# Gated cross-attention with a routed feed-forward: keys loaded in shuffled runs of 128 bytes and turned in 32x32 blocks on VectorE

## The chip, the cores and the metric

The kernel runs on one core of one Trainium2 chip. The time is the device time of one execution in microseconds (us). A profile of one execution stands beside it; times in it are counted from its first instruction. The engines are called as the profile calls them: PE (TensorE, matrix products; PEld is its loading of weights), DVE (VectorE), ACT (ScalarE), POOL (GpSimd), SP (the queue that issues most DMAs). SBUF is the on-chip memory, PSUM the accumulators that PE writes.

## What is computed

All data are float32. There are 32 batches of 128 tokens with 128 features.

```
q    = layernorm(x)                      # x: (32, 128, 128)
k, v = split(ctx, 2)                     # ctx: (32, 128, 256)
w    = softmax(q_h k_h / sqrt(8) + b + mask(seq_len))     # 16 heads of 8
x    = x + tanh(g_xattn) * (w v_h)
y    = layernorm(x)
x    = x + tanh(g_ffn) * sum over the 2 chosen of 8 experts of
       gate * (relu(y wi + bi + (y A_e) B_e) wo + bo)     # hidden 512, rank 16
```

`b` is one number per key, and the mask adds -1e12 to keys at or behind the batch's length.

## The kernel before, in words

**Tiles and groups.** A tile has 128 partitions. Batches come in groups of four: `load(g)` (L191) brings x, the keys and the values of a group (`xg`, `kg`, `vg`, 256 KB each) with one DMA each; group 0 comes in two parts, first batch 0 (`True`), then the other three (`False`, whose keys are issued from ACT, L202). x and keys arrive with tokens on partitions. `load(1)` and `load(2)` are issued ahead of the first steps, `load(3)` inside them, and one more at each group from the fifth on.

**Attention of one batch n**, by the names of the steps:

- `moments0` (L336, DVE) and `query_scale` (L326 to L331, POOL) make the layernorm's factors; `normalise` (L419, ACT) writes the scaled query into `qpad`, where every head has 16 columns: 8 features, and extra ones that carry the key's bias and, later, the row's maximum.
- `key_features` (L381) and `key_bias` (L389) write keys and bias into `kpad` in the same form. In the loop both are part of `group_keys` on POOL.
- `turn` (L444, PE) makes four 128x128 transposes by products with the identity: two of the keys, two of the queries. `turned` (L450, ACT) copies all four from PSUM into `kq`; `keys` (L430, POOL) multiplies the keys' half by a mask into `ks`, so that one strip of 32 rows holds two heads.
- `logits` (L469, PE) makes query times key for one half of the heads in strips of 32 rows, into the one PSUM tile `lg`; `max` (L479, DVE) takes each row's maximum from it. `again` (L488, PE) turns the maxima, `queries` (L495, DVE) adds them to the queries, and a second set of products (L508, PE), with keys on the rows, goes into the one PSUM tile `lt`. `exp` (L537, ACT) reads that, `attend` (L549, PE) multiplies by the values, `attended` (L557, ACT) copies, `result` (L564, PE) turns, `residual` (DVE) divides by the sum and adds x.
- `products` (L469 and L508) interleaves the logits of a batch with the second products of one two batches earlier.

The feed-forward of four batches (steps from `tokens` to `result_out`) runs in the same loop, one group behind. Its products are L620, L635, L726, L737 and L789.

**The order** is written out by hand, and each engine executes its instructions in that order. `START` (L38) lists all until batch 4, `PLAN` (L71) the eight half-ticks that repeat for every four batches, `END` (L117) the rest. Steps of `START` carry their own numbers; the number after a loop step's name is the half, the piece or the group offset. `idle` (L230) are products of zeros that keep PE busy while it would wait; `blank_keys`, `blank_queries` and `blank_values` (L267 to L282) are memsets of the padded tiles, of which there are two each; called in `START`, `blank_values` 0 and all others but `blank_values` 1 run on DVE. The second number of `key_features` and `key_bias` in `START` names the engine: 0 DVE, 1 ACT, 2 POOL.

## Time and profile before

| | before |
|---|---|
| time, median of 3 | 298.6 us (298.49 to 299.34) |
| span of the profiled execution | 296.7 us |
| what the median has beyond that span | 1.9 us |
| PE busy | 286.7 us (97%), 3476 instructions |
| DVE busy | 211.6 us (71%), 592 instructions |
| ACT busy | 162.8 us (55%), 287 instructions |
| POOL busy | 128.1 us (43%), 264 instructions |
| DMA | 9.86 MB in 19109 packets |

Only the span of the profiled execution is recorded, not a total time of its own; the median lies 1.9 us above it, and that is taken as what lies around it. The page of the profile gives busy times and counts of each engine, the span in 40 slices, the DMA queues, the chain of work that ended last with the share of each engine and line, and the costliest groups of instructions. The trace answers further: a timeline of an engine, who waited for whom, and the busy time of each engine in chosen stretches. A matmul's shown duration includes its way through the array, so two neighbours overlap; what one costs PE is the distance between two starts.

### The profile page before, as it was taken

What the parts mean: (1) busy time and instruction counts of PE and PEld (TensorE: products, weight loads), DVE (VectorE), ACT (ScalarE), POOL (GpSimd) and SP (SyncE); (2) the same over time, 40 slices, a digit from 0 to 9 for tenths busy, and PEclk for the clock granted to TensorE, in tenths of its full rate; (3) what the DMA queues carried; (4) which work ended last, traced back from release to release, by engine and by line L of the source; (5) the groups of instructions that cost most, each with busy time, mean ns of one, the idle gap of its engine ahead of it and who ended that gap; (6) DMA issues with size and microseconds to landing.
All of it is one profiled execution on the core that took longest, in us unless ns stands there. A gap on an engine that the chain in (4) does not pass through costs nothing.

```text
span 296.7 us, 8420 instructions
## 1 busy us (share of the span) xinstructions
PE 286.7 (97%) x3476; PEld 209.5 (71%) x3476; DVE 211.6 (71%) x592; ACT 162.8 (55%) x287; POOL 128.1 (43%) x264
## 2 busy tenths in 40 slices
PE   8698999999999999999999999999999999999996
PEld 8477876787666865688567865688666865686475
DVE  7986789788767886777766886777756785348524
ACT  2537675675656654674655644674655643653340
POOL 4792374263624436353634436343633035304620
PEclk9999999999999999999999999999999999999999
DMA  5990003000400000050001000010001000011001
GB/s 138 271 244 12 2 3 106 2 4 0 127 2 0 2 2 2 0 144 4 2 0 38 3 2 0 2 39 2 0 2 38 2 0 3 1 38 35 2 0 53
DMA packets 19109, 9.86 MB, mean 33 GB/s; under 512 B 1664, under 2 KB 18816, under 8 KB 19072
## 3 DMA queue, kind: packets, MB, share of 16 engines
q1 hardware_dynamic: 18384, 9.12, 11.1%
q8 instruction: 27, 0.44, 0.6%
q10 hardware_dynamic: 688, 0.21, 0.3%
q14 instruction: 10, 0.08, 0.1%
HBM read 7.24 MB, written 2.10 MB: 31 GB/s over the span
## 4 chain that ended last, share of the span: by engine, by line
PE 88%; DVE 5%; DMA 2%; ACT 1%; POOL 1%; issue 1%; SPq 0%; ACTq 0%
PE ph L737 26%; PE lg L469 13%; PE lt L508 11%; PE shared L549 10%; PE po L789 10%; PE pt L444 4%; PE pzt L726 3%; PE pz L635 2%; PE avt L564 2%; PE shared L488 2%; DMA len_i<-in_seq_len_dram 1%; DVE highest L479 1%; DMA xg<-in_x_dram 1%; PE px L620 1%; PE busy L230 1%
## 5 line engine op out<-in xcount | busy, mean ns | idle before, releaser
L479 DVE TENSOR_REDUCE highest<-lg 128x8 f32<-128x1024 f32 x64 | 77.8, 1218 | 20.0 <-PE lt L508 13.9
L537 ACT ACTIVATE e<-lt 128x1024 f32<-128x1024 f32 x64 | 65.6, 1025 | 35.1 <-PE lt L508 34.6
L508 PE MATMUL lt<-qm,ks 32*128 32x128 f32 x1024 | 74.2, 283 | 0.2 <-ACT e L537 0.2
L469 PE MATMUL lg<-ks,kq 32*128 32x256 f32 x512 | 71.0, 400 | 0.2
L508 PEld LDWEIGHTS lt<-qm,ks 32*128 32x128 f32 x1024 | 62.0, 186 | 2.2 <-issue 1.4
L430 POOL TENSOR_TENSOR ks<-kq,head_mask 128x512 f32<-128x512 f32 x32 | 33.3, 1042 | 64.1 <-ACT kq L450 64.0
L737 PE MATMUL ph<-zt,bt_sb 128*128 128x512 f32 (+1 forms) x128 | 58.3, 568 | 0.0
L469 PEld LDWEIGHTS lg<-ks,kq 32*128 32x128 f32 x512 | 42.9, 184 | 19.5 <-issue 11.5
L781 DVE SCALAR_TENSOR_TENSOR h<-ph,nbi,r 128x512 f32<-128x512 f32 (+1 forms) x32 | 22.7, 708 | 21.2 <-PE ph L737 20.8
L789 PE MATMUL po<-wo_sb,h 128*128 128x128 f32 x256 | 35.0, 283 | 0.0
L549 PE MATMUL shared<-e,values 128*32 128x128 f32 x1024 | 34.6, 276 | 0.2 <-ACT e L537 0.2
L789 PEld LDWEIGHTS po<-wo_sb,h 128*128 128x128 f32 x256 | 30.9, 191 | 2.3
L737 PE MATMUL ph<-xt,wi_sb 128*128 128x512 f32 (+1 forms) x64 | 32.3, 589 | 0.0
L767 ACT ACTIVATE r<-ph,bi_sb 128x512 f32<-128x512 f32 (+1 forms) x32 | 21.2, 663 | 19.6 <-PE ph L737 19.6
L737 PEld LDWEIGHTS ph<-zt,bt_sb 128*128 128x128 f32 x128 | 21.8, 190 | 14.1 <-issue 11.2
L549 PEld LDWEIGHTS shared<-e,values 128*32 128x32 f32 x1024 | 26.0, 109 | 6.0 <-issue 3.2
L714 POOL TENSOR_TENSOR zm<-z,hot 128x512 f32<-128x512 f32 (+1 forms) x18 | 17.4, 966 | 26.4 <-DVE hot L686 17.6
L450 ACT COPY kq<-pt 128x512 f32<-128x512 f32 x32 | 18.7, 586 | 10.1 <-PE pt L444 9.9
L557 ACT COPY avs<-shared 128x256 f32<-128x256 f32 x32 | 11.9, 371 | 17.4 <-PE shared L549 16.8
L495 DVE TENSOR_TENSOR qm<-kq,shared 128x256 f32<-128x256 f32 x32 | 13.2, 413 | 11.2 <-ACT avs L557 10.4
L419 ACT ACTIVATE qpad<-xg,sh_q,rs_q 128x128 f32<-128x128 f32 x32 | 14.9, 493 | 7.7 <-POOL sh_q L331 7.1
L733 ACT COPY zt<-pzt 128x512 f32<-128x512 f32 (+1 forms) x18 | 9.7, 537 | 15.0 <-PE pzt L726 15.0
(121 smaller groups left out, 386.6 us busy)
## 6 DMA issues: line engine op xcount, KB each, us to landing
vg<-in_ctx_dram SPq DMA_DIRECT2D x8, 256.0 KB, 4.7
xg<-in_x_dram SPq DMA_DIRECT2D x7, 256.0 KB, 4.0
kg<-in_ctx_dram SPq DMA_DIRECT2D x7, 256.0 KB, 4.4
out_dram<-y SPq DMA_DIRECT2D x7, 256.0 KB, 2.3
wi_sb<-in_wi_t_dram SPq DMA_DIRECT2D x1, 256.0 KB, 4.9
wo_sb<-in_wo_t_dram SPq DMA_DIRECT2D x1, 256.0 KB, 5.2
bt_sb<-in_b_t_dram SPq DMA_DIRECT2D x1, 256.0 KB, 4.6
xg<-in_x_dram SPq DMA_DIRECT2D x1, 192.0 KB, 4.3
```

The lines of the kernel that those rows point to most:

```text
L430: engine.tensor_tensor(dst, src.unsqueeze(2).to_broadcast([P, 2, HB, P]), head_mask.unsqueeze(1).unsqueeze(3).to_broadcast([P, 2, HB, P]), ...
L450: nc.scalar.copy(kq, T.pop("pt"))
L469: lambda r=slice(32 * s, 32 * s + 32), d=lg[:, s % 2, c], c=c: nc.tensor.matmul(d, lhsT=T["kq"][r, 2 + c, :], rhs=T["ks"][r, c], start=Tru ...
L479: nc.vector.tensor_reduce(highest[n % 2][:, :, DH : DH + 2].rearrange("p (s j) c -> p s c j", s=NS)[:, 2 * half : 2 * half + 2], lg, AX.X, ...
L508: lambda r=slice(32 * s, 32 * s + 32), d=lt[:, s % 2, c, j], c=c, j=j: nc.tensor.matmul(d, lhsT=T["ks"][r, c, j, :], rhs=T["qm"][r, c, :], ...
L537: nc.scalar.activation(e, lt.rearrange("p s c j q -> p (s c j) q"), AF.Exp)
L549: nc.tensor.matmul(shared[32 * j : 32 * j + 32, 0, half, :], lhsT=group[g]["v"][:, i, HH * c + HB * s + odd, :], rhs=e[:, 2 * j + odd, :], ...
L714: nc.gpsimd.tensor_tensor(zm.rearrange("p b (e r) -> p (b e) r", r=R), G["z"][:, :nb].rearrange("p b (e r) -> p (b e) r", r=R), G[f"hot{k} ...
L737: nc.tensor.matmul(G["ph", c], lhsT=weights[:, c * P : (c + 1) * P], rhs=rows[:, : G["nb"]].rearrange("p b t -> p (b t)"), **flags)
L767: nc.scalar.activation(r, G["ph", c], AF.Relu, bias=bi_sb[:, c : c + 1])
L781: nc.vector.scalar_tensor_tensor(G["h"][:, c, : G["nb"] * P], G.pop(("ph", c)), nbi[:, c : c + 1], G.pop(("r", c)), ALU.max, ALU.add)
L789: nc.tensor.matmul(po, lhsT=G["h"][:, c, i * P : (i + 1) * P], rhs=wo_sb[:, c, :], start=(c == 0), stop=(c == NFC - 1),)
```

## The change

Keys are no longer turned by PE. Their DMA is split into four, one for each strip of 32 partitions. Within strip s, partition 32s+c receives for every batch the four runs of 32 consecutive features number s (128 bytes) of the keys c, 32+c, 64+c and 96+c. So each 32x32 block of the padded keys needs only to be turned in place, which the new step `turn_keys` does with one VectorE transpose of 128x256 elements a batch into `kt`. `turn` keeps the two transposes of the queries, `turned` copies half as much into `qt`, and `keys` on POOL reads `kt`. The bias of the keys follows the new layout: it is loaded by four DMAs and computed for four blocks. The queries' heads are laid out in the order of the strips, so `attend` and `result` address them differently, with the same number of instructions. All three lists of steps are ordered anew.

```diff
START = [
-    ("blank_queries", 1), ("blank_keys", 1), ("moments0", 0), ("lengths",), ("biases",),
-    ("key_features", 0, 0, 1, 4), ("query_scale", 0, 0, 1), ("key_features", 0, 1, 0, 1),
-    ("moments0", 1), ("query_scale", 0, 1, 2), ("key_bias", 0, 1, 0, 1), ("normalise", 0),
-    ("turn", 0), ("key_bias", 0, 0, 1, 4), ("moments0", 2), ("turned", 0),
-    ("normalise", 1), ("moments0", 3), ("keys", 0), ("turn", 1), ("blank_values", 0), ("idle", 1),
-    ("products", (0, 0, False), (0, 1, False)), ("query_scale", 0, 2, 4), ("turned", 1),
-    ("moments0", 6), ("moments0", 4), ("keys", 1), ("moments0", 5), ("max", 0, 0), ("normalise", 2),
-    ("turn", 2), ("normalise", 3), ("max", 0, 1), ("turned", 2), ("turn", 3),
-    ("products", (1, 0, False)), ("keys", 2), ("tanh",), ("moments0", 7), ("turned", 3),
-    ("max", 1, 0), ("group_keys", 1), ("normalise", 5), ("products", (1, 1, False)), ("max", 1, 1),
-    ("again", 0), ("normalise", 4), ("idle", 2), ("products", (2, 0, False)), ("queries", 0),
-    ("idle", 1), ("products", (0, 1, True)), ("again", 1), ("max", 2, 0), ("exp", 0, 1),
-    ("turn", 4), ("queries", 1), ("products", (2, 1, False), (0, 0, True)), ("exp", 0, 0),
...
+    ("moments0", 0), ("lengths",), ("biases",), ("key_bias", 0, 1, 0, 1), ("moments0", 1),
+    ("moments0", 3), ("query_scale", 0, 0, 1), ("key_bias", 0, 0, 1, 4),
+    ("key_features", 0, 1, 0, 1), ("key_features", 0, 0, 1, 4), ("turn_keys", 0), ("turn_keys", 1),
+    ("normalise", 0), ("query_scale", 0, 1, 2), ("keys", 0), ("turn", 0), ("turned", 0),
+    ("normalise", 1), ("idle", 1), ("products", (0, 0, False), (0, 1, False)), ("moments0", 2),
+    ("blank_keys", 1), ("query_scale", 0, 2, 4), ("normalise", 3), ("moments0", 6), ("turn", 1),
+    ("keys", 1), ("normalise", 2), ("moments0", 5), ("load", 3), ("idle", 4), ("turn", 2),
+    ("turn_keys", 2), ("max", 0, 1), ("idle", 1), ("max", 0, 0), ("turned", 1), ("moments0", 7),
+    ("blank_values", 0), ("again", 0), ("products", (1, 0, False)), ("max", 1, 0), ("tanh",),
+    ("keys", 2), ("queries", 0), ("turned", 2), ("products", (1, 1, False)), ("max", 1, 1),
+    ("turn", 3), ("blank_values", 1), ("moments0", 4), ("products", (2, 0, False)), ("max", 2, 0),
+    ("products", (0, 1, True)), ("turned", 3), ("group_keys", 1), ("exp", 0, 1), ("turn_keys", 3),
+    ("group_values", 0), ("blank_queries", 1), ("again", 1), ("normalise", 5),
+    ("products", (2, 1, False), (0, 0, True)), ("normalise", 4), ("queries", 1), ("turn", 5),
+    ("max", 2, 1), ("turn_keys", 4), ("idle", 2), ("exp", 0, 0), ("moments0", 10), ("keys", 3),
+    ("turn", 4), ("products", (3, 0, False), (1, 1, True)), ("again", 2), ("exp", 1, 1),
+    ("attend", 0), ("normalise", 6), ("moments0", 11), ("keys", 4), ("attended", 0), ("max", 3, 0),
+    ("moments0", 8), ("queries", 2), ("turn_keys", 5), ("products", (3, 1, False), (1, 0, True)),
+    ("turned", 4), ("keys", 5), ("max", 3, 1), ("turn_keys", 6), ("result", 0), ("exp", 1, 0),
+    ("products", (4, 0, False), (2, 1, True)), ("residual", 0), ("again", 3), ("attend", 1),
+    ("max", 4, 0), ("queries", 3), ("turned", 5), ("exp", 2, 1), ("keys", 6), ("attended", 1),
+    ("moments0", 9), ("products", (4, 1, False), (2, 0, True)), ("moments1", 0), ("normalise", 7),
+    ("result", 1), ("max", 4, 1), ("residual", 1), ("turn", 6), ("output_bias",), ("exp", 2, 0),
+    ("moments1", 1), ("products", (5, 0, False), (3, 1, True)), ("again", 4), ("exp", 3, 1),
+    ("group_values", 1), ("scale", 0), ("max", 5, 0), ("turned", 6), ("attend", 2),
+    ("products", (5, 1, False), (3, 0, True)), ("attended", 2), ("token", 0, 1), ("queries", 4),
+    ("token", 0, 0), ("exp", 3, 0), ("result", 2), ("tokens", 0), ("idle", 1), ("max", 5, 1),
+    ("group_keys", 2), ("residual", 2), ("idle", 1), ("moments1", 2),
 ]
...
 PLAN = [
     [
...
+        ("again",), ("logits", 0), ("tokens_sb", 1), ("moments0",),
     ],
     [
...
+        ("turn_keys",), ("attend",), ("project", 1, 0), ("max", 0), ("gates", 1, 0), ("exp", 1),
+        ("attended",), ("project", 1, 1), ("queries",), ("project_sb", 1, 0), ("gates", 1, 1),
+        ("out", 2, 2), ("result",), ("keys",), ("logits", 1), ("scores", 1), ("result_out", 2, 2),
+        ("exps", 1), ("residual",), ("project_sb", 1, 1), ("turn",), ("normalise",),
+        ("softmax", 1), ("turned",), ("exp", 0), ("out", 2, 1), ("max", 1), ("choice", 1, 0),
+        ("result_out", 2, 1), ("moments1",),
     ],
     [
...
+        ("common", 1, 1), ("turn",), ("turned",), ("masked", 1, 0), ("normalise",), ("logits", 0),
+        ("exp", 1), ("max", 0), ("attend",), ("choice", 1, 1), ("features", 1, 0), ("attended",),
+        ("common", 1, 0), ("again",), ("features_sb", 1, 0), ("masked", 1, 1), ("result",),
+        ("residual",), ("turn_keys",), ("keys",),
     ],
     [
...
+        ("logits", 1), ("features", 1, 1), ("own", 1, 1), ("moments0",), ("max", 1), ("own", 1, 0),
+        ("features_sb", 1, 1), ("relu", 1, 1), ("common", 1, 3), ("queries",), ("exp", 0),
+        ("relu", 1, 0), ("own", 1, 3), ("moments1",),
     ],
     [
...
+        ("second", 1, 1), ("logits", 0), ("relu", 1, 3), ("weight", 1), ("sum", 1, 1),
+        ("bias", 1, 1), ("again",), ("moments0",), ("bias", 1, 2), ("normalise",), ("turn",),
+        ("exp", 1), ("second", 1, 0), ("attend",), ("max", 0), ("logits", 1), ("turned",),
+        ("turn_keys",),
     ],
     [
...
+        ("sum", 1, 0), ("attended",), ("bias", 1, 0), ("exp", 0), ("queries",), ("result",),
+        ("max", 1), ("common", 1, 2), ("own", 1, 2), ("residual",), ("keys",), ("moments1",),
     ],
     [
...
+        ("normalise",), ("second", 1, 3), ("group_values", -1), ("again",), ("relu", 1, 2),
+        ("bias", 2, 3),
     ],
     [
...
+        ("out", 2, 3), ("result_out", 2, 3), ("scale", 0), ("logits", 0), ("turn_keys",),
+        ("max", 0), ("attend",), ("exp", 1), ("sum", 1, 3), ("keys",), ("turn",), ("second", 1, 2),
+        ("attended",), ("token", 0, 0), ("token", 0, 1), ("logits", 1), ("moments0",), ("turned",),
+        ("sum", 1, 2), ("queries",), ("max", 1), ("result",), ("token", 0, 2), ("group_keys", -2),
+        ("residual",), ("token", 0, 3), ("out", 1, 0), ("result_out", 1, 0), ("exp", 0),
+        ("tokens", 0), ("moments1",),
     ],
 ]
...
         bs = slice(g * GB + part.start, g * GB + part.stop)
         nc.sync.dma_start(out=xg[:, part, :], in_=x[bs].rearrange("b s d -> s b d"))
         keys = nc.scalar if first is False else nc.sync
-        keys.dma_start(out=kg[:, part, :], in_=ctx_kv[bs, :, 0:D].rearrange("b s d -> s b d"))
+        for s in range(NS):
+            keys.dma_start(
+                out=kg[32 * s : 32 * s + 32, part, :].rearrange("c n (b r) -> c n b r", r=32),
+                in_=ctx_kv[bs, :, 32 * s : 32 * s + 32].rearrange("n (b c) r -> c n b r", c=32),
+            )
         if first is not True:
             bs = slice(g * GB, (g + 1) * GB)
...
 
     len_i = const.tile([P, B], I32, name="len_i")
     nc.scalar.dma_start(out=len_i, in_=seq_len.to_broadcast([P, B]))
-    b_key = const.tile([P, 1], FP, name="b_key")
-    nc.scalar.dma_start(out=b_key, in_=b_col)
+    b_key = const.tile([P, NS], FP, name="b_key")
+    for s in range(NS):
+        nc.scalar.dma_start(
+            out=b_key[32 * s : 32 * s + 32, :], in_=b_row.rearrange("o (b c) -> c (o b)", c=32)
+        )
     load(0, True)
...
     nc.vector.tensor_copy(row, row_i)
-    pidx = const.tile([P, 1], FP, name="pidx")
-    nc.vector.tensor_copy(pidx, pidx_i)
+    pidx = const.tile([P, NS], FP, name="pidx")
+    nc.gpsimd.iota(pidx, [[32, NS]], base=0, channel_multiplier=0, allow_small_or_imprecise_dtypes=True)
+    nc.vector.tensor_scalar(pidx, pidx, row, None, ALU.add)
 
     head_mask = const.tile([P, HB], FP, name="head_mask")
...
-        kpads.append(const.tile([P, GB, H, HS], FP, name=f"kpad{i}"))
-        qpads.append(const.tile([P, GB, H, HS], FP, name=f"qpad{i}"))
+        kpads.append(const.tile([P, GB, NS, NS, HS], FP, name=f"kpad{i}"))
+        qpads.append(const.tile([P, GB, 2, NS, HB, HS], FP, name=f"qpad{i}"))
         values.append(const.tile([P, GB, H, 32], FP, name=f"values{i}"))
 
...
         for c in range(2):
-            engine.memset(kpads[i][:, :, c * HH : (c + 1) * HH, DH + c], 1.0)
+            engine.memset(kpads[i][:, :, :, HB * c : HB * c + HB, DH + c], 1.0)
 
     def blank_queries(engine, i):
         engine.memset(qpads[i], 0.0)
-        engine.memset(qpads[i].rearrange("p b h c -> p (b h) c")[:, :, DH + 2], 1.0)
+        engine.memset(qpads[i].rearrange("p b c s j e -> p (b c s j) e")[:, :, DH + 2], 1.0)
 
...
-        nc.vector.tensor_scalar(bias_key, len_f, pidx, MASK_VALUE, ALU.is_le, ALU.mult)
-        nc.vector.tensor_scalar(bias_key, bias_key, b_key, None, ALU.add)
-        nc.vector.tensor_tensor(bias_key, bias_key, some, ALU.mult)
+        def wide(t, axis):
+            return t.unsqueeze(axis).to_broadcast([P, B, NS])
+
+        nc.vector.tensor_tensor(bias_key, wide(len_f, 2), wide(pidx, 1), ALU.is_le)
+        nc.vector.scalar_tensor_tensor(
+            bias_key, bias_key, MASK_VALUE, wide(b_key, 1), ALU.mult, ALU.add
+        )
+        nc.vector.tensor_tensor(bias_key, bias_key, wide(some, 2), ALU.mult)
 
...
         G = record(g)
         copy = (nc.vector.tensor_copy, nc.scalar.copy, nc.gpsimd.tensor_copy)[engine]
         copy(
-            G["k"][:, lo:hi].rearrange("p b h c -> p (b h) c")[:, :, 0:DH],
+            G["k"][:, lo:hi].rearrange("p n b h c -> p (n b h) c")[:, :, 0:DH],
             G["kg"][:, lo:hi].rearrange("p b (h e) -> p (b h) e", e=DH),
         )
...
         copy(
-            record(g)["k"][:, lo:hi, :, DH + 2],
-            bias_key[:, n].unsqueeze(2).to_broadcast([P, hi - lo, H]),
+            record(g)["k"][:, lo:hi, :, :, DH + 2].rearrange("p n b h -> p (n b) h"),
+            bias_key[:, n].rearrange("p n b -> p (n b)").unsqueeze(2).to_broadcast(
+                [P, (hi - lo) * NS, NS]
+            ),
         )
 
     def query_scale(g, lo=0, hi=GB):
...
         G = group[g]
         nc.scalar.activation(
-            G["q"][:, i, :, 0:DH], G["xg"][:, i, :].rearrange("p (h e) -> p h e", e=DH),
+            G["q"][:, i, :, :, :, 0:DH],
+            G["xg"][:, i, :].rearrange("p (s c j e) -> p c s j e", c=2, j=HB, e=DH),
             AF.Identity, scale=G["rs"][:, i : i + 1], bias=G["sh"][:, i : i + 1],
         )
...
         g, i = divmod(n, GB)
         G = group[g]
-        pt = small([P, 4, P], f"pt{n}")
-        for s, t in enumerate((G["k"], G["q"])):
-            for c in range(2):
-                nc.tensor.transpose(pt[:, 2 * s + c, :], half_of(t, i, c), ident)
-        batch[n] = dict(pt=pt)
+        pt = small([P, 2, P], f"pt{n}")
+        for c in range(2):
+            heads = G["q"][:, i, c].rearrange("p s j e -> p (s j e)")
+            nc.tensor.transpose(pt[:, c, :], heads, ident)
+        batch.setdefault(n, {})["pt"] = pt
 
     def turned(n):
         T = batch[n]
-        kq = bat.tile([P, 4, P], FP, tag="kq", name=f"kq{n}", bufs=5)
-        nc.scalar.copy(kq, T.pop("pt"))
-        T["kq"] = kq
+        qt = bat.tile([P, 2, P], FP, tag="qt", name=f"qt{n}", bufs=5)
+        nc.scalar.copy(qt, T.pop("pt"))
+        T["qt"] = qt
+
+    def turn_keys(n):
+
+        g, i = divmod(n, GB)
+        kt = bat.tile([P, 2, P], FP, tag="kt", name=f"kt{n}", bufs=3)
+        nc.vector.transpose(
+            kt.rearrange("p c (b t) -> p b c t", t=32),
+            group[g]["k"][:, i].rearrange("p b (c j) e -> p b c (j e)", j=HB),
+        )
+        batch.setdefault(n, {})["kt"] = kt
 
     def keys_by_head(n):
         ks = bat.tile([P, 2, HB, P], FP, tag="ks", name=f"ks{n}", bufs=5)
-        spread(nc.gpsimd, ks, batch[n]["kq"][:, 0:2, :])
+        spread(nc.gpsimd, ks, batch[n].pop("kt"))
         batch[n]["ks"] = ks
 
 
...
-                    d, lhsT=T["kq"][r, 2 + c, :], rhs=T["ks"][r, c], start=True, stop=True
+                    d, lhsT=T["qt"][r, c, :], rhs=T["ks"][r, c], start=True, stop=True
                 )
                 for c in range(2)
...
-                    s, c = 2 * half + j // 2, j % 2
                     nc.tensor.matmul(
                         shared[32 * j : 32 * j + 32, 0, half, :],
-                        lhsT=group[g]["v"][:, i, HH * c + HB * s + odd, :], rhs=e[:, 2 * j + odd, :],
+                        lhsT=group[g]["v"][:, i, HH * half + HB * j + odd, :], rhs=e[:, 2 * j + odd, :],
                         start=(odd == 0), stop=(odd == 1),
                     )
...
         avt = small([P, 4, P], f"avt{n}")
         for half in range(2):
-            nc.tensor.transpose(
-                avt[:, 0:2, 64 * half : 64 * half + 64].rearrange("p c (s e) -> p s c e", e=32),
-                batch[n]["avs"][:, half, :], ident,
-            )
+            nc.tensor.transpose(avt[:, half, :], batch[n]["avs"][:, half, :], ident)
         batch[n]["avt"] = avt
 
```

Where the diff shows "...", lines are left out: the rest of the old `START`, the old `PLAN`, both `END`s, and changes of shape that only follow the new layout.

## The prediction

> **What bounds the kernel now.** I read the page first, then the busy time by stage, then PE's timeline, then who waits on SP's queue. The page and the stages:
>
> ```profile
> span 296.7 us, 8420 instructions
> PE 88%; DVE 5%; DMA 2%; ACT 1%; POOL 1%; issue 1%; SPq 0%; ACTq 0%
> ```
> ```profile
> core 0: us, PE busy (x) PEld busy (x) DVE busy (x) ACT busy (x) POOL busy (x), PEclk, DMA share, GB/s
> 0.00:11.04 11.04, 8.08 (x43) 7.30 (x43) 8.43 (x31) 3.72 (x8) 6.05 (x24) 1.00 0.74 192
> 11.04:39.16 28.12, 25.52 (x381) 20.36 (x380) 22.02 (x49) 16.68 (x29) 16.46 (x32) 1.00 0.37 101
> 39.16:250.72 211.56, 211.13 (x2716) 151.46 (x2715) 158.35 (x438) 125.20 (x217) 92.94 (x178) 1.00 0.07 19
> 250.72:296.70 45.98, 42.00 (x341) 30.41 (x340) 22.78 (x77) 17.21 (x34) 12.68 (x30) 1.00 0.07 21
> ```
>
> The stages are: until the first logits, the rest of `START`, the loop, `END`. In the loop PE is busy 211.13 of 211.56 us: there PE's own work sets the pace, and DVE has 25% to spare. Before 39.16 it is otherwise; PE waits there although `idle` products fill part of the gaps.
>
> PE's timeline at one `turn` among other full-size products:
>
> ```profile
> 134.24 1.05 PE L789 MATMUL po<-wo_sb,h 128*128 128x128 f32 x8
> 135.13 0.38 PE L444 MATMUL pt<-ident,kpad 128*128 128x128 f32 x2
> 135.34 0.38 PE L444 MATMUL pt<-ident,qpad 128*128 128x128 f32 x2
> 135.56 0.38 PE L564 MATMUL avt<-ident,avs 128*128 128x128 f32 x2
> ```
>
> Starts are what counts: the keys' pair costs 135.34 - 135.13 = 0.21 us, the queries' 0.22, so one transpose 0.11.
>
> SP's waits:
>
> ```profile
> SPq L217 <- DMA len_i<-in_seq_len_dram: 1.5, 1, 1.5
> SPq L314 <- DMA vg<-in_ctx_dram: 0.6, 1, 0.6
> SPq L201 <- DMA wi_sb<-in_wi_t_dram: 0.5, 1, 0.5
> SPq L203 <- DMA wo_sb<-in_wo_t_dram: 0.5, 1, 0.5
> ```
>
> Number the DMAs in program order: 1 `len_i`, 2 `b_key`, 3 and 4 x and keys of batch 0, 5 to 7 the rest of group 0, 8 and 9 the gates (L216, L217), and so on. L217 (9) waits for `len_i` (1), L314 (20) for the values of group 1 (12), x of group 2 (21) for `wi_sb` (13), its keys (22) for `wo_sb` (14). Each DMA that waits, waits for the eighth before it. I read eight slots in turn out of that: more DMAs at the start mean later DMAs.
>
> **The loop: what PE saves.** `turn` loses two transposes a batch, 0.218 us. The loop turns batches 7 to 31, 25 of them: 25 x 0.218 = **5.45 us**. The number of PE blocks is the same in both `PLAN`s (I count 8 of `products`, 4 of `attend` and 8 of full-size work between them), so no switch is gained or lost; I take nothing for it. A period of four batches (112.31 to 145.91 in the chain, 33.60 us) should become 33.60 - 0.87 = 32.73.
>
> **The loop: what must fit beside it.**
>
> - The DVE transpose is in no row. The nearest are the copy of 128x384 (353 ns), `qm` of 128x256 (413 ns) and the memset of 1024 elements (912 ns, so 0.23 us for 256). I take 0.35, nearest in shape; the lower end is 0.23, the upper 1.2, what the slowest step of a batch, L479 with 1218 ns, takes. DVE has 24.9 us in a period; with four transposes 26.3 of 32.73, at the upper end 29.7. It is in DVE's queue ahead of `max` twice, once of those in time that DVE waits for the product anyhow. By PE's order the second logits of the first half-ticks come 4.5 us into the period, and that `max` would be done at 3.1: 1.4 us of room, which even 1.2 us leaves.
> - ACT's `turned` falls from 586 to about 371 ns (the row of the 128x256 `avs`); POOL's `ks` stays at 1042. Both are cover, and gain nothing.
> - Tight places: `choice` ends on DVE at about 8.6 us of the period, POOL's `masked` (1.06) at 9.8, and `features` is due on PE at 10.1; the next pair is as close (12.8 and 13.1). `max` before the third `products` ends at 7.4, due at 8.0. They fit by 0.3 to 0.6 us, so I take no stall; if all three miss by 0.3 us, 7 periods lose about 6 us.
> - Keys of later groups are loaded a dozen ticks ahead. A packet of 512 bytes cost 0.111 x 16 x 296.7 / 18384 = 28.7 ns of one DMA engine. 128 bytes cost between a quarter of that and all of it: 0.9 to 3.7 us for a group on 16 engines, against 0.9 now, hidden in the loop.
>
> **The start: what it costs.** There three DMAs become twelve. In the new order: 1 `len_i`, 2 to 5 `b_key` (ACT), 6 x of batch 0, 7 to 10 its keys (SP), 11 the other x, 12 to 15 their keys (ACT), 16 values, 17 and 18 the gates, 19 x of group 1. Before, landing took 3.0 us for x of batch 0, 3.7 for its keys, 3.9 for `len_i` and `b_key`, 4.3 and 4.6 for the other x and keys, with 784 KB under way at once. Fewer bytes are under way now, so I take 3.5 for small ones; ends 3.0 and the rows as they are. Issuing takes 0.45 each.
>
> 1. `len_i` lands at 4.5, `b_key` at 4.7 to 6.1. Keys of batch 0, parts 3 and 4, wait for slots 1 and 2: issued 4.5 and 4.9, landed 8.2. The other x waits for slot 3: issued 5.3, landed 9.3. The other keys wait on ACT for slots 4 to 7: issued 5.8 to 7.1, landed 10.8. ACT's table load (1.28) stands behind them and ends near 8.9, in time.
> 2. On DVE `key_features` of batches 1 to 3 stands ahead of `turn_keys` of batch 0. So 10.8 + 0.35 + 0.35 + `ks` 1.04 + 0.1 = 12.6 for the first logits, against 11.04: 1.6 us late.
> 3. Three memsets that DVE did while it waited (by 11.3 us) have moved among its work. `blank_keys` still fits. x of group 1 (slot of 11: issued 9.4, landed 13.5) holds two `moments0` (0.4 each) and `turn_keys` ahead of the first maximum: 14.7. Two maxima (1.15 each), `moments0`, `blank_values` (1.76 and 0.2), then max, `queries` (0.35), max: 22.0. The second products of batch 0 need 1.1, so its first `exp` starts at 23.3, against 19.45.
> 4. From there logits and maximum take turns on the one `lg`. The trace has such steps 2.47 us apart (22.70 to 25.17, 28.93 to 31.39, 33.98 to 36.45), and 2.6 to 3.8 between batches, where PE waited for other steps. `normalise` of batch 5 waits for `blank_queries` (1.03) and costs 0.35 once. Logits of (3,0) at 26.9, then six steps of 2.5: (6,0), the loop's first, at 41.9 to 42.2, against 39.16. **Start: 3.0 us later.**
>
> Bounds of this: 1.5 with landings of 3.0 and the best turn-taking, 4.5 with the landings as the rows have them.
>
> The TensorE clock is 1.00 in every stage of the table, and there is no PE gap over 1.0 us after 7.4. After the change PE has nothing from 7.4 to about 10. The Trainium skill ("TensorE: Matmul & The Clock Gate", Part 1) says that the clock halves after an idle window of about 3.4 us; by that the first logits could run at half speed, an estimate of 1 us more. No trace here shows it, and I add nothing.
>
> The same skill speaks against the loading ("DMA: Bandwidth & Descriptors", Rules for kernel authors): transfers to separate partition ranges share the same engines, so one transfer should be used, and runs under 512 bytes miss line rate. It gives no price for 128 bytes from HBM to a strip; the packet bounds above stay my measure, and in the loop (DMA share 0.07) neither matters.
>
> **`END`** has the same PE work in another order, no turning. PE idles 4.0 us there, about 2.9 of them behind its last product. A better order could save 0.8, a worse one lose as much; I take nothing.
>
> **The sum.** Against the span: 296.7 - 5.45 + 3.0 = 294.25; with the 1.9 us around it **296.2 us**.
>
> **Rivals.**
>
> - *The start costs little* (landings near 3.0, `START` ordered well, `END` better by 0.5): 298.6 - 5.45 + 0.8 - 0.5 = 293.4. For it: PE has 2.6 us without work from 11.04 to 39.16 and `idle` products besides, which a better order could use. Against it: the memsets on DVE's path.
> - *Slow slots: slower.* If a 128-byte packet costs as much as a 512-byte one, the 1536 packets of the other keys take 1536 x 28.7 / 16 = 2.8 us instead of 0.7, those of batch 0 0.9 instead of 0.2, and each later DMA waits for a slot held that long: first logits near 15.4 and the start 5.8 to 7 us late. It decides from a start of 5.45 us late, so (6,0) at 44.6. Time: 298.6 - 5.45 + 7 = 300.2.
> - *The loop does not keep up*: the tight places miss, PE waits in every period, and the 5.45 us are given back with the start's 3.0 on top: up to 301. Against it: DVE's 25%; for it: rooms of 0.3 us on in-order queues.
> - *The change does not do what it says*: PE's starts show the keys' pair as real cost, so only a transpose on DVE far beyond 1.2 us would undo it. I give it no chance of its own.
>
> **Chances.** Forecast (294.6 to 298) 0.50, cheap start 0.17, slow slots 0.20, loop not keeping up 0.13. Faster by over 0.3% (below 297.7; about what a measurement of this kernel can tell from no change): 0.45 of the first and all of the second, 0.62. Within: 0.05 of the first, 0.04 each of the last two, 0.13. Slower (above 299.5): 0.25. The range 293.0 to 300.8 reaches into all of them.
>
> **What will show it.** `pt` 64 instead of 128 transposes and 6 to 7 us less of L444; a period of 32.7 us with PE busy throughout (loop right), or PE waits at `pzt` or `lg` (wrong). The first logits near 12.6 and (6,0) near 42; SP and ACT DMAs waiting for the eighth before. A DVE transpose over 1.2 us, a landing over 5 us at the start or a lower clock before 16 us would make the number wrong.

## The result, and the profile after

The changed kernel takes 299.24 us (median of 20 executions, 298.4 to 300.46), the kernel before 298.53 (20 executions, 298.36 to 299.4): a ratio of 1.0023, with a 95% interval of 1.0013 to 1.0034. It is slower by a quarter of a per cent. The forecast was 296.2 and faster: wrong in sign, though inside the range. The profiled execution (298.61 us) has a span of 296.8, 0.1 above that of before, while the medians differ by 0.7; the stages below split the two profiled executions. From its page, the span, the shares of the chain that ended last, and the clock in 40 slices:

```profile
span 296.8 us, 8403 instructions
PE 78%; DVE 12%; DMA 3%; POOL 2%; issue 2%; ACT 1%; ACTq 0%; DVEq 0%
PEclk9665999999999999999999999999999999999999
```

The span is that of before, but its parts are not: DVE's share of the chain went from 5% to 12%, and slices two to four (7.4 to 29.7 us) have a TensorE clock of half to two thirds. Before it was full there. The same four stages as in the prediction, busy time by engine:

```profile
core 0: us, PE busy (x) PEld busy (x) DVE busy (x) ACT busy (x) POOL busy (x), PEclk, DMA share, GB/s
0.00:13.34 13.34, 7.26 (x37) 6.78 (x37) 6.16 (x28) 2.94 (x7) 5.99 (x25) 0.85 0.66 127
13.34:45.81 32.47, 29.63 (x372) 23.47 (x372) 27.02 (x59) 15.06 (x29) 17.46 (x35) 0.80 0.45 100
45.81:251.18 205.37, 203.56 (x2680) 146.99 (x2680) 163.15 (x462) 119.63 (x219) 91.30 (x176) 1.00 0.08 19
251.18:296.83 45.65, 41.79 (x327) 29.39 (x326) 22.63 (x77) 16.77 (x33) 12.66 (x30) 0.99 0.07 21
```

The loop fell from 211.56 to 205.37 us (-6.19) and `END` from 45.98 to 45.65 (-0.33). The start grew by 45.81 - 39.16 = 6.65: 2.30 until the first logits, 4.35 behind them. -6.52 and +6.65 are all of the difference between the two spans.

In the loop PE is still the bound, and the DVE transpose fits. PE's timeline at two `turn`s, and the groups of `kt` and its reader:

```profile
140.08 0.44 PE L457 MATMUL pt<-ident,qpad 128*128 128x128 f32 x2
140.35 1.06 PE L808 MATMUL po<-wo_sb,h 128*128 128x128 f32 x8
...
142.10 0.38 PE L457 MATMUL pt<-ident,qpad 128*128 128x128 f32 x2
142.41 0.48 PE L492 MATMUL lg<-ks,qt 32*128 32x256 f32 x2
```
```profile
L470 DVE STREAM_TRANSPOSE kt<-kpad x32: 404/434/439, 11.7 to 233.1; 128x256 f32<-128x256 f32 x32
L443 POOL TENSOR_TENSOR ks<-kt,head_mask x32: 1038/1039/1042, 12.2 to 233.7; 128x512 f32<-128x512 f32 x32
```

Only the queries' pair is left. The transpose takes 0.43 us (minimum, median and maximum in ns), where the forecast took 0.35. The period of four batches, from one turn of the maxima (`again`) to the fourth after it, is 134.42 - 101.89 = 32.53 us, from 33.60; 32.73 was forecast.

The start is another matter. The chain of waits there (start, length, what):

```profile
1.15 3.19 DMA b_key<-in_b_row_dram
4.36 3.60 DMA kg<-in_ctx_dram
7.97 3.39 DMA kg<-in_ctx_dram
11.40 0.04 issue
11.45 0.06 DVE kpad L395
11.51 0.21 issue
11.72 0.45 DVE kt L470
12.18 0.07 issue
12.24 1.05 POOL ks L443
13.34 2.13 PE lg L492 x16
...
15.56 2.36 DVE highest L502 x2
...
18.71 1.76 DVE values L286
```

Three transfers follow each other, the second and third held until their slot's earlier transfer lands. The view puts the third down to a transfer that went out at 7.97; by the landing times it is the last part of the keys of batches 1 to 3, issued at 7.71 and landed at 11.26, in the slot of the rest of x (4.12 to 7.69), which had itself waited for the first part of batch 0's keys (1.17 to 4.11). Then comes DVE's copy for batches 1 to 3, which batch 0's transpose stands behind; and at 18.71 `blank_values` on DVE, ahead of the queries of the second products. PE's timeline in the same stretch (in brackets: idle time before it, and what ended it), and below it the first logits of the kernel before:

```profile
3.76 3.42 PE L238 MATMUL busy<-idle 128*128 128x128 f32 x20
10.30 0.69 PE L457 MATMUL pt<-ident,qpad 128*128 128x128 f32 x2 [3.12 <-ACT qpad L435]
...
13.34 2.09 PE L492 MATMUL lg<-ks,qt 32*128 32x256 f32 x16 [1.92 <-POOL ks L443]
...
23.34 2.07 PE L531 MATMUL lt<-qm,ks 32*128 32x128 f32 x16 [0.23 <-DVE highest L502]
```
```profile
11.04 1.15 PE L469 MATMUL lg<-ks,kq 32*128 32x256 f32 x16
```

The 16 logits that took 1.15 us before take 2.09. The trace's records of the clock come in pieces of 3.41 us (called windows here): 0.5 from 9.31 to 19.55 and from 22.96 to 29.79, five windows. Before, the record is 1.0 from 6.43 to 296.56.

One more number serves below: the start of PE's turn of the maxima that stands last ahead of the loop's logits (6, 0), called **the turn** from here on. It is 38.91 before and 45.56 after. From there to the last instruction it is 257.8 us before and 251.3 after; the table shows that this rest hardly moves while the loop is left alone, so the turn measures the start.

### The profile page after: what moved, and what is told of

Same layout as the page of the kernel before. It is cut to its first block, busy times and chain, and to the rows that moved or that the text cites. A ratio compares the mean times of both kernels' runs of the same rounds, so it can differ in the third digit from the quotient of the medians.

```text
span 296.8 us, 8403 instructions
## 1 busy us (share of the span) xinstructions
PE 282.3 (95%) x3412; PEld 206.6 (70%) x3412; DVE 219.0 (74%) x624; ACT 154.4 (52%) x287; POOL 127.4 (43%) x265
## 4 chain that ended last, share of the span: by engine, by line
PE 78%; DVE 12%; DMA 3%; POOL 2%; issue 2%; ACT 1%; ACTq 0%; DVEq 0%
PE ph L756 24%; PE lg L492 12%; PE lt L531 11%; PE shared L571 10%; PE po L808 8%; DVE highest L502 4%; PE pzt L745 3%; PE avt L586 2%; DMA kg<-in_ctx_dram 2%; PE pz L654 2%; PE pt L457 2%; PE shared L511 2%; DMA b_key<-in_b_row_dram 1%; POOL zm L733 1%; PE px L639 1%
## 5 line engine op out<-in xcount | busy, mean ns | idle before, releaser
L492 PE MATMUL lg<-ks,qt 32*128 32x256 f32 x512 | 72.5, 416 | 5.5 <-POOL ks L443 1.9
L531 PE MATMUL lt<-qm,ks 32*128 32x128 f32 x1024 | 76.1, 287 | 0.2 <-DVE highest L502 0.2
L531 PEld LDWEIGHTS lt<-qm,ks 32*128 32x128 f32 x1024 | 63.7, 190 | 2.8 <-ACT r L786 0.8
L492 PEld LDWEIGHTS lg<-ks,qt 32*128 32x128 f32 x512 | 43.8, 193 | 24.1 <-issue 7.4
L443 POOL TENSOR_TENSOR ks<-kt,head_mask 128x512 f32<-128x512 f32 x32 | 33.2, 1039 | 48.1 <-DVE kt L470 47.7
L808 PE MATMUL po<-wo_sb,h 128*128 128x128 f32 x256 | 33.1, 275 | 0.0
L756 PE MATMUL ph<-xt,wi_sb 128*128 128x512 f32 (+1 forms) x64 | 31.0, 567 | 0.0
L463 ACT COPY qt<-pt 128x256 f32<-128x256 f32 x32 | 11.8, 368 | 14.1 <-PE pt L457 14.0
L820 DVE SCALAR_TENSOR_TENSOR y<-po,w,x 128x128 f32<-128x128 f32 x32 | 11.0, 347 | 10.9 <-PE po L808 10.9
L457 PE MATMUL pt<-ident,qpad 128*128 128x128 f32 x64 | 14.2, 306 | 3.1 <-ACT qpad L435 3.1
```

The source lines that it names most:

```text
L443: engine.tensor_tensor(dst, src.unsqueeze(2).to_broadcast([P, 2, HB, P]), head_mask.unsqueeze(1).unsqueeze(3).to_broadcast([P, 2, HB, P]), ...
L457: nc.tensor.transpose(pt[:, c, :], heads, ident)
L492: lambda r=slice(32 * s, 32 * s + 32), d=lg[:, s % 2, c], c=c: nc.tensor.matmul(d, lhsT=T["qt"][r, c, :], rhs=T["ks"][r, c], start=True, s ...
L531: lambda r=slice(32 * s, 32 * s + 32), d=lt[:, s % 2, c, j], c=c, j=j: nc.tensor.matmul(d, lhsT=T["ks"][r, c, j, :], rhs=T["qm"][r, c, :], ...
L756: nc.tensor.matmul(G["ph", c], lhsT=weights[:, c * P : (c + 1) * P], rhs=rows[:, : G["nb"]].rearrange("p b t -> p (b t)"), **flags)
L808: nc.tensor.matmul(po, lhsT=G["h"][:, c, i * P : (i + 1) * P], rhs=wo_sb[:, c, :], start=(c == 0), stop=(c == NFC - 1),)
```

## The experiments

After the result the theories were: **C**, the halved clock; **L**, the extra transfers; **M**, the memsets on DVE's path; later **O**, the order of batch 0's work on DVE and POOL. All times in us; ratios are to the kernel before as it ran beside each run (medians 298.53 to 299.18), with 95% intervals.

| run | at clock 0.5 before 40 us | first logits | the turn | rest | time | ratio |
|---|---|---|---|---|---|---|
| before | 0 | 11.04 | 38.91 | 257.8 | 298.53 | 1 |
| after | 17.1 | 13.34 | 45.56 | 251.3 | 299.24 | 1.0023 (1.0013 to 1.0034) |
| e1_warm | 10.2 | 13.32 | 46.02 | 251.3 | 299.12 | 1.0005 (0.9987 to 1.0023) |
| e2_early | 13.7 | 13.26 | 44.83 | 251.3 | 297.87 | 0.9975 (0.9959 to 0.9991) |
| e3_onedma | 10.2 | 9.62 | 42.53 | 251.6 | 295.61 | 0.9877 (0.9842 to 0.9911) |
| e4_both | 10.2 | 13.45 | 44.84 | 251.3 | 296.76 | 0.9938 (0.9916 to 0.9959) |
| e5_clock | 0 | 13.16 | 41.48 | 251.3 | 295.10 | 0.9864 (0.9843 to 0.9885) |
| e6_best | 0 | 10.64 | 40.12 | 251.2 | 293.13 | 0.9802 (0.9785 to 0.9820) |
| e7_pekeys | 13.7 | 13.50 | 45.90 | 256.1 | 304.40 | 1.0181 (1.0151 to 1.0210) |
| e8_dvetwice | 13.7 | 13.27 | 45.72 | 252.2 | 300.75 | 1.0062 (1.0038 to 1.0086) |
| e9_steady_onedma | 0 | 14.01 | 42.33 | 251.5 | 296.10 | 0.9912 (0.9899 to 0.9925) |
| e10_hybrid | 10.2 | 11.22 | 42.83 | 251.6 | 295.74 | 0.9887 (0.9852 to 0.9923) |
| e11_cold | cold until 14.2 | 11.23 | 38.24 | 257.8 | 298.22 | 0.9983 (0.9974 to 0.9992) |
| e12_hybrid_steady | 0 | 11.71 | 38.55 | 253.1 | 291.96 | 0.9773 (0.9760 to 0.9786) |
| e13_best_onedma | 0 | 10.89 | 40.36 | 251.3 | 293.64 | 0.9836 (0.9814 to 0.9858) |

First logits, turn and rest are of the profiled execution, the time is the median. Where the clock falls differs from one execution of a program to the next, so medians also hold executions with other windows.

### Four first attempts at the start

**e1_warm**, more `idle` products:

```diff
-NIDLE = 16
+NIDLE = 27
-    ("normalise", 1), ("idle", 1), ("products", (0, 0, False), (0, 1, False)),
+    ("normalise", 1), ("idle", 8), ("products", (0, 0, False), (0, 1, False)),
```

> The changed kernel with more products of zeros before the first logits (27 at the very start for 16, and 8 for 1 after the first turn), so that PE has no gap over 0.5 us between 1.0 and 13.3 us; nothing else differs. Theory C (clock): the gap from 7.2 to 10.3 us lowers the TensorE clock to 0.5, and the half-speed products cost 3 to 4 us of the start: clock 1.00 from 6 us on, first logits still near 13.3, logits (6,0) near 42.3 for 45.8, time 295.0 to 296.5. Theory L (loading: DMA slots and small packets make the start late): first logits at 13.3 as before, (6,0) at 45 or later, time within 0.7 of 299.2. Theory M (memsets on DVE's path): as L.

**e2_early**, the memsets where DVE waits for transfers (they leave their later places in the list):

```diff
-    ("moments0", 0), ("lengths",), ("biases",),
+    ("moments0", 0), ("lengths",), ("blank_queries", 1), ("blank_keys", 1), ("biases",),
-    ("key_bias", 0, 0, 1, 4),
+    ("key_bias", 0, 0, 1, 4), ("blank_values", 0),
```

> The changed kernel with the three memset steps on DVE moved into waits that DVE has anyway (blank_queries 1 and blank_keys 1 ahead of biases, blank_values 0 ahead of key_features); nothing else differs. Theory M: the maxima of batch 1 no longer wait for 1.9 us of memset, nor queries of batch 1 for 1.0: (6,0) 2 to 3 us earlier, time 296.2 to 297.2. Theory C: the clock still falls, PE's slow products take the place of the memset: time 298.2 to 299.2. Theory L: first logits unchanged at 13.3, time within 0.5 of 299.2.

**e3_onedma**, group 0's keys as before in one DMA a part, and `b_key` in one; keys and biases of group 0 are then in the wrong places, so only the time is read:

```diff
-        for s in range(NS):
+        if g == 0:
+            keys.dma_start(out=kg[:, part, :], in_=ctx_kv[bs, :, 0:D].rearrange("b s d -> s b d"))
+        for s in range(NS if g else 0):
```

> The changed kernel with group 0's keys loaded as before the change, by one DMA in rows of 512 bytes for batch 0 and one for the others, and the bias of the keys by one DMA; so the output is not the reference's (keys of group 0 and all biases are in the wrong places). Theory L: first logits near 11.4 for 13.3, and the end 1.9 us earlier or more, time 297.3 or less. Theory C: the first turn comes about 2 us earlier, so the gap shrinks to some 1 to 1.5 us and the clock may stay up: then 2 us for the loading and 3 to 4 for the clock, 293 to 294.5; if the clock still falls, 297 to 298. Theory M: the memsets stay, so no less than 296.

**e4_both** is e1 and e2 together.

> The edits of e1_warm and e2_early together. Theory C with M beside it: 5 to 6.5 us less than the changed kernel, 293 to 294.3, (6,0) near 40. Theory C alone: as e1_warm, 295.0 to 296.5. Theory L: within 0.7 of 299.2.

e1 shortened the gap it was aimed at from 3.12 to 1.72 us, and the clock fell later instead: at 0.5 from 21.03 to 31.27, the turn no earlier. So five windows became three without any gain. That fits windows that cost little while PE waits for others anyway, and e1 could not decide about C. e2's memsets are worth 45.56 - 44.83 = 0.73 us of the turn (1.37 by medians), with four windows for five. e3 has its first logits 3.7 us earlier and the turn 3.03 earlier, with the clock still falling in three windows. No theory's numbers hold for all four: e3's 295.61 lies below what M allowed (296), e4's 296.76 above what C alone did (295.0 to 296.5). None of these runs held the clock.

### The clock alone

**e5_clock** is e4 with more `idle` products at the four places where PE still waited:

```diff
-    ("moments0", 4), ("products", (2, 0, False)),
+    ("moments0", 4), ("idle", 4), ("products", (2, 0, False)),
-    ("products", (0, 1, True)),
+    ("idle", 1), ("products", (0, 1, True)),
-    ("products", (2, 1, False), (0, 0, True)),
+    ("idle", 2), ("products", (2, 1, False), (0, 0, True)),
-    ("turn_keys", 4), ("idle", 2),
+    ("turn_keys", 4), ("idle", 4),
```

> The run with early memsets and more idle products (296.76), with further idle products ahead of the products of (2, 0), (0, 1) and (2, 1) and four in place of two ahead of batch 4, so that no window of the start is left thin on TensorE. Nothing else is changed. Theory C (the half clock sets part of the start): the records stay at 1.0 through the start, the three windows at 0.5 (10.2 us) go, the loop's first logits come 2 to 3.5 us earlier than after that run's 44.84, 41.3 to 42.8, and the time is 293.3 to 294.8. Rival (the start is set by transfers, POOL and DVE, and TensorE waits for these at either clock): the logits stay at 44.5 to 45 and the time within 0.5 us of 296.8.

The stretch 20 to 30 us by busy time, first of e4, then of e5:

```profile
20.00:30.00 10.00, 9.98 (x79) 8.54 (x81) 6.01 (x13) 2.81 (x4) 4.75 (x9) 0.51 0.91 185
```
```profile
20.00:30.00 10.00, 9.98 (x150) 8.01 (x147) 8.06 (x18) 5.06 (x9) 4.79 (x10) 1.00 1.14 190
```

PE is busy 9.98 us in both, with 79 products at clock 0.51 and 150 at 1.00. This is how a fallen clock looks: the busy time shows nothing, the count and the clock column do. The turn comes at 41.48 instead of 44.84, 3.36 us earlier. Of that, 0.29 is there at the first logits already (13.16 against 13.45), ahead of e4's fall of the clock at 20.19. The rest, **3.1 us, is the price of three windows in which PE was the bound**. The medians differ by less, 1.66 us: four of e4's five executions have a mean clock of 0.988, worth two windows, and only the profiled one has three; e5's four are all at 1.0. Adding work to PE made the kernel faster. C holds, for that much; the time expected, 293.3 to 294.8, was met by the profiled execution (294.52) and missed by the median (295.10).

### The order

**e6_best** adds to e5's filling a new front of `START`: the keys of batches 1 to 3 are issued from SP, everything on batch 0's keys stands ahead of what waits for batches 1 to 3, and both `blank_values` are on POOL; ahead of the first logits it has fewer `idle` products (20 for 27, and 3 for 8).

```diff
-    ("key_features", 0, 1, 0, 1), ("key_features", 0, 0, 1, 4), ("turn_keys", 0), ("turn_keys", 1),
-    ("normalise", 0), ("query_scale", 0, 1, 2), ("keys", 0), ("turn", 0), ("turned", 0),
+    ("biases",), ("key_bias", 0, 1, 0, 1), ("key_features", 0, 1, 0, 1), ("query_scale", 0, 0, 1),
+    ("turn_keys", 0), ("keys", 0), ("moments0", 1), ("moments0", 3), ("moments0", 2),
...
+    ("max", 0, 1), ("key_features", 0, 0, 1, 4), ("turn_keys", 1), ("max", 0, 0), ("normalise", 3),
```

> The run before with the front of the start reordered: the keys' transfers of batches 1 to 3 are issued from SP instead of ACT, all the work on batch 0's keys (bias, features, transpose, masked copies) stands ahead of any instruction that waits for batches 1 to 3, both blank_values are on POOL, and the first maximum stands ahead of the features of batches 1 to 3. Theory O (a good part of the loss is order: on DVE and POOL batch 0's keys stand behind instructions that wait for batches 1 to 3, landed at 11.3): first logits at 9 to 10 instead of 13.3, the loop's first logits at 37 to 40, time 290 to 292.5. Rival L (the number of loads through eight slots sets the start, whatever the order): first logits at 12 or later, and the time within 1 us of that of the run before.

The first logits come at 10.64 (9 to 10 was expected), the turn at 40.12, just outside the 37 to 40 expected, and 293.13 us. O is worth 41.48 - 40.12 = 1.36 us (1.97 by medians), less than expected.

### The loop

**e7_pekeys** gives PE the two key transposes back, unread; **e8_dvetwice** does the DVE transpose twice.

```diff
+        if n >= 7:
+            for c in range(2):
+                heads = G["k"][:, i, 2 * c : 2 * c + 2].rearrange("p b h e -> p (b h e)")
+                nc.tensor.transpose(pt[:, 2 + c, :], heads, ident)
```

> The changed kernel, where TensorE makes the two key transposes by the identity as well, from batch 7 on; nothing reads their result, and the output is unchanged. Theory (in the loop TensorE is the bound and each such product costs its own time): the period from one loop pass to the next goes from 32.53 to 33.3 to 33.6 us, and the time up by 5 to 6.5 us to 304 to 306. Rival (the loop's gain comes from elsewhere, such as the smaller copy out of PSUM on ACT): the period stays under 32.9 and the time under 302.

```diff
-        nc.vector.transpose(
+        for _ in range(2 if n >= 7 else 1):
+          nc.vector.transpose(
```

> The changed kernel with the 32x32-block transpose of the keys done twice on DVE from batch 7 on; output unchanged. Theory (DVE has room in the loop: it is busy 74% of the span): the period stays at 32.5 to 32.7 and the time within 1 us of 299.2. Rival (the transpose stands in the way of the masked copies and features, so that its time goes onto the path): 0.41 to 0.45 us more a batch, 1.7 a period, 10 to 11 us in all.

e7's period is 136.86 - 103.45 = 33.41 us, 0.88 more for eight products, 0.11 each: the reading of PE's starts was right. Its rest grows by 4.8 us, of the 6.5 that the change gained. The other 1.7 are not the two products; they come with the new order of `PLAN` and `END`, or with what e7 leaves as it is (ACT still copies only the queries' half). That split was not tried. e8's period is 135.50 - 102.98 = 32.52, unchanged: in the steady loop DVE has room for twice the transpose. Its rest is 0.9 longer, 0.5 of it in the first four batches behind the turn and 0.4 in the next four; its time is 1.5 us above that of the changed kernel, where at most 1 was expected.

### Transfers and memsets stand in for one another

**e9_steady_onedma** is e5 with e3's edit, **e13_best_onedma** is e6 with it; in both, as in e3, keys and biases of group 0 lie in the wrong places.

> The run with the clock held at 1.0 (294.52 profiled, last pass of the maxima's turn before the loop's logits at 41.48), with group 0's keys by one DMA a part in rows of 512 bytes and b_key by one DMA; it puts keys and bias of group 0 in the wrong places, so only its time is read. Theory L (the four-part loads cost 3 us of the start by themselves, not through the clock): the turn at 38.0 to 39.0, time 291.5 to 292.5. Rival (the loads mattered because they made TensorE idle and halved its clock): the turn at 40.8 to 41.5, time within 0.7 us of 294.5.

> The reordered run (293.13, clock 1.0, turn at 40.12) with group 0's keys by one DMA a part in rows of 512 bytes and b_key by one DMA; it puts keys and bias of group 0 in the wrong places, so only its time is read. Theory L (the extra transfers are worth something of their own when order and clock are right): first logits at 8.5 to 9.5 instead of 10.64, the turn at 38.3 to 39.3, time 291.2 to 292.3. Rival (behind the first logits POOL and DVE set the start, whatever arrives earlier): the turn at 39.7 to 40.2, time 292.7 to 293.2.

With the keys' transfers early, e9 is slower than e5 (the turn at 42.33 against 41.48) and e13 no faster than e6 (40.36 against 40.12). L fell in its pure form, and the rivals' numbers for the turn were missed too, by 0.8 and 0.2 us. DVE's timelines show why, first of e6, then of e13:

```profile
5.15 0.91 DVE L282 MEMSET qpad<- 128x1024 f32 x1
...
6.43 0.91 DVE L277 MEMSET kpad<- 128x1024 f32 x1
...
8.07 0.29 DVE L390 TENSOR_TENSOR bias_key<-bias_key,some 128x128 f32<-128x128 f32 x1
9.02 0.45 DVE L470 STREAM_TRANSPOSE kt<-kpad 128x256 f32<-128x256 f32 x1 [0.66 <-ACT kpad L395]
```
```profile
5.46 0.91 DVE L282 MEMSET qpad<- 128x1024 f32 x1 [0.16 <-issue]
...
6.74 0.91 DVE L277 MEMSET kpad<- 128x1024 f32 x1
...
8.38 0.29 DVE L390 TENSOR_TENSOR bias_key<-bias_key,some 128x128 f32<-128x128 f32 x1
9.27 0.45 DVE L470 STREAM_TRANSPOSE kt<-kpad 128x256 f32<-128x256 f32 x1 [0.60 <-ACT kpad L395]
```

DVE has hardly a gap in either. In e6 the last part of `b_key` lands at 6.61, while the memsets run; in e13 `b_key` is there at 5.07, but the bias that needs it still stands behind them, so that all 2 us of memsets lie on the path. And the row begins later: the lengths and x of batch 0, with which DVE starts, land at 4.66 and 4.44 in e13 and at 3.79 and 3.51 in e6, where smaller transfers follow them. In e9 and e5 it is the same (5.06 and 4.83 against 3.84 and 3.68). e3, where the memsets came later, gained 3.03 us from the same loads. In this start a late transfer is a place to put 2 us of memsets; that an early one is worth something when they stand elsewhere was not tried at full clock.

### The change in the loop alone, and the kernel before without idle products

**e10_hybrid** keeps batches 0 to 3 as before (plain loads, products by the identity, the old `START`) and changes batches 4 to 31. **e12_hybrid_steady** adds `idle` products and moves the shuffled bias and group 1's features off DVE's first passes. **e11_cold** is the kernel before with its `idle` products taken out.

```diff
+        pt = small([P, 2 if g else 4, P], f"pt{n}")
+        for c in range(0 if g else 2):
+            heads = kplain[:, i, c].rearrange("p s j e -> p (s j e)")
+            nc.tensor.transpose(pt[:, 2 + c, :], heads, ident)
```

> The change in the loop alone: batches 0 to 3 as in the kernel before (keys by one DMA a part, products by the identity, the start's steps in the order of before), batches 4 to 31 as in the changed kernel, with a plain copy of the padded keys and a plain bias for group 0, and the DMAs of the shuffled bias moved behind the transfers of group 1. Theory (the change gains about 6.5 us in the loop and loses them in the start): the turn ahead of the loop's logits at 38.9 to 40, from there on as the changed kernel, 291.8 to 293. Rival (the changed loop needs the changed start: the shuffled keys of batches 4 to 6 come late behind the older order): 294 or more.

e12 against e10:

```diff
-NIDLE = 16
+NIDLE = 22
-    ("turn", 0),
+    ("turn", 0), ("idle", 3),
-    ("keys", 0), ("turn", 1), ("blank_values", 0), ("idle", 1),
+    ("keys", 0), ("idle", 4), ("turn", 1), ("blank_values", 0), ("idle", 2),
-    ("biases",), ("max", 1, 0), ("group_keys", 1),
+    ("max", 1, 0), ("query_scale", 1),
-    ("max", 2, 0), ("exp", 0, 1),
+    ("max", 2, 0), ("biases",), ("key_features", 1, 2), ("key_bias", 1, 2), ("exp", 0, 1),
```

> The run with the change in the loop alone, with six more idle products at the head and eight between the first products, and the shuffled bias and the features of group 1 moved behind the maximum of (2, 0), off DVE's path to the first passes. Theory C (that run's 296.19 was the clock: 0.5 in three windows, one execution at 1.0 took 292.8): the records stay at 1.0, the turn ahead of the loop's logits goes from 42.83 to 38.9 to 40, time 291.5 to 293. Rival: the turn stays above 41.5 and the time above 294, since the old start with the new loop waits for DVE and transfers.

e11 against the kernel before:

```diff
-NIDLE = 16
+NIDLE = 1
-    ("idle", 1),
...
```

> The kernel before with its idle products taken out (one product left of the 16 at the head, none between the steps); nothing that is read is changed. Theory C (a window of 3.41 us at half the clock costs the start about 1.1 us, as 3.36 us came back with three windows): three to seven windows at 0.5 before 40 us, the turn ahead of the loop's logits at 42 to 46 instead of 38.91, time 302 to 306. Rival (the kernel before waits for transfers in its start, and TensorE's clock does not matter there): the turn within 1 us of 38.91 and the time within 1 us of 298.5.

e10's median missed its expectation (295.74 us, the turn at 42.83), and its executions say why. The profiled one has three windows at 0.5 and takes 296.19 us. Another of the same program, at clock 1.000, takes 292.8. That is 3.4 us again, and no instruction differs. Two with a mean clock of 0.987 to 0.988, worth two windows, take 295.28 and 295.29, 2.5 us more than at 1.000. e12 has the turn at 38.55, a little ahead of what was expected, and the best time of all: 291.96, ratio 0.9773 (0.9760 to 0.9786). Its stretch from 8 to 12 us, where before PE was busy 2.42 of 4 us:

```profile
8.00:12.00 4.00, 3.95 (x36) 3.60 (x38) 3.39 (x14) 2.16 (x4) 3.30 (x11) 1.00 0.71 119
```

The profiled execution of e12 lost one window inside the loop, from 47.08 to 50.50; hence its rest of 253.1 and its 293.38, where the others took 291.85 to 292.11.

e11 went against its expectation. There is no record of the clock before 14.19, where it comes up to 1.0 and stays; until then the products are slow (2.09 us for the 16 first logits, as in the changed kernel). The turn is 0.67 us earlier and the time 0.3 us shorter. In the kernel before the `idle` products bought nothing. Half clock before 14 us is cheap, since PE waits there; it is dear from 20 to 30 us.

## Why the prediction was wrong

- **The loop** (-5.45 from two transposes at 0.109): right in mechanism, too small. PE had 211.13 of 211.56 us busy before and 203.56 of 205.37 after. e7 prices the transposes at 4.8 us, less than 5.45: the period of the first four batches behind the turn grew by 0.43 instead of 0.88, and the last ones by less too; the other 1.7, which the forecast took at nothing, lie in the order of `PLAN` and `END` or in what e7 left as it was.
- **What must fit beside it** (no stall in the tight places, a DVE transpose of 0.35): right; 0.43, and e8 shows room for 0.87 in the steady loop. So the loop kept up; the rival that it would not is refuted (its price is 298.6 + 3.0 = 301.6, not 301).
- **`END` at nothing**: it gave 0.33.
- **Slots.** Eight slots in turn was right, but they go by the order of issue on both queues, not by the program's numbering: the first held transfer, the last part of batch 0's keys, waited for x of batch 0 (landed 3.71) and went out at 3.73. The last of batches 1 to 3 had the slot of x's rest, landed 7.69, and itself landed at 11.3, not 10.8. First logits 13.34 against 12.6.
- **Memsets on DVE's path**: right in place (`blank_values` at 18.71 in the chain, first `exp` 25.45 instead of 23.3). Moving them away was worth 0.73 us (e2), a quarter of the 3 us that the forecast counted for them.
- **The clock: the step that failed.** "No trace here shows it, and I add nothing." The gap of PE from 7.4 to 10 was seen (7.18 to 10.30 in the trace), its consequence was weighed and set to zero, although a lower clock before 16 us stood among the signs of a wrong number. The records show five windows at 0.5, the first from 9.31; taking away the three that were left in e4 was worth 3.1 us (e5), most of the 3.65 between the forecast start of +3.0 and the measured +6.65. An estimate of the changed kernel's time without the fall, 296.8 - 3.1 + 1.9 = 295.6, lies 0.6 below the forecast; the loop and `END` gave 1.1 more than it counted on (6.52 against 5.45). The five windows of the changed kernel were not taken away by themselves; the price is that of e4's three, with the memsets already moved.
- **From logits (3,0) on**: right. Six steps of 2.5 us were to lead from (3,0) to (6,0); they took 45.81 - 30.15 = 15.66 us, against 15.0 to 15.3. What the start lost beyond the forecast it lost ahead of them: (3,0) came at 30.15 instead of 26.9. At full clock, with the memsets moved, it comes at 26.07, and (6,0) at 41.73, where 41.9 to 42.2 was forecast. The first products of (3,0), in the changed kernel and in e5:

```profile
30.15 0.48 PE L492 MATMUL lg<-ks,qt 32*128 32x256 f32 x2
```
```profile
26.07 0.48 PE L492 MATMUL lg<-ks,qt 32*128 32x256 f32 x2
```

- **Rivals.** "Slow slots" named 300.2, nearest to the result, and its sign, (6,0) later than 44.6, came true; its mechanism did not. It had the first logits near 15.4 (measured 13.34) and longer transfers, but the parts of the keys of batches 0 to 3 landed 2.1 to 4.8 us after issue, against 3.7 and 4.6 for the whole loads before. That it comes so near is luck. "The start costs little", 293.4, supposed a start ordered well: with that and a clock at 1.0, e6 measured 293.13.

On the clock, the trace differs from the page that the prediction weighed. The Trainium skill ("TensorE: Matmul & The Clock Gate", Part 1) gives an idle window of about 3.4 us as the condition for half clock. In e4 the clock fell at 20.19 after a window (16.78 to 20.19) in which PE was busy 60% (2.04 of 3.41 us), with no gap over 1.1 us. The length of the pieces, 3.41 us, agrees.

Of the +6.65 us, then: 3.36 is what e5 gained on e4, 3.1 of it the clock, 0.72 the memsets (after to e4), 1.36 batch 0's order (e5 to e6), and 1.57 what remains between e6 and e12, which has the old start for group 0. That sums to 7.01, since e12's turn is 0.36 ahead of the kernel before. By medians the same steps are 2.48 (after to e4), 1.66, 1.97 and 1.17 us; they hold executions with other numbers of windows. These are steps of one sequence; as transfers and memsets stand in for one another, another sequence would divide them otherwise. What share of busy time makes the clock fall stays open: windows with 47% in e9 and 54% in e5 were followed by full clock, one with 89% in e2, behind one with 69%, by half. Neither busy share nor the longest gap sorts them all.

## What to carry to other kernels

A change that saves PE work in a steady loop may pay for it in the start, where PE waits: split the span at the first logits and at the loop's first step before adding anything up, and price a gap in PE together with the clock of what follows it. Keep a new loading scheme to the batches whose transfers are hidden, and load the first ones the old way (e12: 2.3% faster than before). A busy engine at half clock looks like a busy engine; read the count of instructions and the clock beside it.

## What the runs showed of the hardware

- The TensorE clock changes in pieces of 3.41 us whose phase differs from one execution to the next: the same program (e10) takes 292.8 us at a mean clock of 1.000 and 296.19 at 0.983.
- PE does not have to be idle for a whole piece: 60% busy was followed by half clock in e4. A late, cold start was followed by full clock from 14.19 on (e11).
- The 32x32-block transpose of 128x256 float32 takes 0.43 us on DVE (the changed kernel); the product by the identity costs PE 0.11 us for 128x128, at full clock (e7).
- A transfer of 16 KB in runs of 128 bytes lands 2.1 to 3.3 us after issue (median of four 2.9), one of 192 KB in runs of 512 bytes 3.6 (up to 14 us of the changed kernel): twelve times the bytes take a quarter longer.
- The same first transfer lands later where large ones follow it closely: the lengths (16 KB, issued at 0.7) land at 4.5 to 5.1 us in the seven runs that load group 0's keys whole, and at 3.8 to 4.1 in the eight that load them in parts.
